# Sparse attention on one core: the first sum of W_v formed three units earlier, and its first block loaded through another queue

## The chip, the core and the metric

The kernel runs on one core of a Trainium2 chip. The metric is the device time of one execution in microseconds (us). Of the version before, three timed executions are shown: 629.04, 630.61 and 632.04 us, a median of 630.61 us. One further execution was profiled; it took 627.51 us, of which the trace covers a span of 625.8 us.

## The reference

`x` has 2708 rows of 1024 numbers, `adj` is a 2708 x 2708 matrix of zeros and ones with about 0.15% ones, so a node has some four neighbours. All is float32.

```python
h = jnp.maximum(_layernorm(x, axis=-1), 0.0)
q = h @ W_q.T + b_q
k = h @ W_k.T + b_k
v = h @ W_v.T + b_v
z = (q @ k.T) / sqrt(1024) * adj
z = jnp.where(z == 0.0, -10000.0, z)
x = x + jax.nn.relu(softmax(z, axis=1) @ v)
```

Since a row of `adj` is nearly empty, the softmax needs only the few neighbours of a node. And since the weights of a row sum to one, `v` need not be formed for every node: the neighbours' rows of `h` are summed with their weights, and the sum is multiplied by `W_v` once.

## The kernel before, in words

**Tiles and units.** The nodes are 22 tiles of 128 rows. First TensorE forms M, the product of W_q and W_k with the scale (until about 107 us). Then come 20 units. A unit multiplies two tiles of rows (256 x 1024) by a 1024 x 1024 matrix that lies in SBUF, with Strassen's scheme in Winograd's form: seven block products instead of eight. Units 0 to 9 (kind "q", the last is `last_q`) multiply `h` by M, units 10 to 19 (kind "o") multiply the weighted sums by W_v; a last single tile follows. `FIRST` is 4. Rows are gathered in an order sorted by the number of neighbours, first from unit 4 on; until unit 3 tiles come as they lie.

**The matrix.** `M[:, i, j]` are the four blocks of the matrix and `T[:, k]` (the tile `wlow`) are four sums of blocks. For W_v the names in the code are b11 = `M[:, 0, 0]`, t1 = `M[:, 0, 1]`, b21 = `M[:, 1, 0]`, b22 = `M[:, 1, 1]`. "W_v's first sum" is t1 = W_v(0,1) - W_v(0,0): the block W_v(0,0) is loaded into t1's place, ScalarE negates it there in two halves, and a DMA of GpSimd's queue adds W_v(0,1) on its way in. T1 is then T0 - t1, T2 is T1 - b11, T3 is b21 - T1. A q unit reads `M[:, 0, 0]` and `T[:, 0]` in its first two products and never reads `M[:, 0, 1]`: an o unit reads `M[:, 0, 1]` in the product where a q unit reads `T[:, 0]`. Until the change, `M[:, 0, 1]` of the old matrix has one late reader: the sum of its squares (`squared(1)`, step "g1"), a check on the size of M.

**A unit in order of time** (`multiply`, `opened`, `between`): product s2 x T1 into the bank Y, a12 x b21 into X, s4 x b22 into Z, s3 x T2 into Y; then the next unit is *opened*: its a11 x b11 into a fresh X, a ScalarE copy of X into its Y bank (the line `nc.scalar.copy(Y, X)`), its s1 product into its Z; then this unit's a22 x T3 into the old Y. Between s3 x T2 and a22 x T3 the result c22 is read out of Y: by VectorE itself (line 1097) in units 6 to 9, by a ScalarE copy (`taken`, line 1081) in units 4 and 5 and in the o units. The a22 product cannot start before that read is over.

**The attention stream.** From unit 4 on VectorE works beside the products on the attention: scores (line 863: one neighbour's row times the query's row, summed), weights, and weighted sums (line 923). The neighbours' rows `g` come by indirect DMA of GpSimd's queue from `h_dram` (line 610), the queries' rows `pq` by line 612 or 833. A buffer is refilled when VectorE has done with it. Before that the neighbour table has to be sorted: eight "puts" (line 626, steps "w0-7") write its rows to DRAM, a load of SyncE's queue brings them back (line 638).

**What sets the order.** VectorE's order is written out by hand all along: steps at the places `after(i)`, i from 0 to 6, of each unit, a table `steps_at`, and an allowance of us of attention work for each place. ScalarE's is written out until unit 4 and left to the scheduler after it; `tc.issue_after(x)` binds a step behind another. GpSimd's order is written out between some points (`pooled`). The DMA queues of SyncE, ScalarE and GpSimd are issued in the order of these engines. The finished sums go to `u_dram` through ScalarE's queue and come back as rows `or` in quarters (line 700) through SyncE's.

Of the kernel before, what the change touches and what calls it, by code (L numbers as in the profile page):

```python
# [14 lines left out]
AF = mybir.ActivationFunctionType  # L15
ALU = mybir.AluOpType
AX = mybir.AxisListType

P = 128
NB = 512  # L20
# [3 lines left out]
SLOTS = 16  # L24
# [41 lines left out]
def tile_preln_masked_attention(  # L66
# [686 lines left out]
    placed = []  # L753

    def banks_for(row):

        return_ = []
        for h in range(NH):
            return_.append(psum.tile([P, NB], FT, tag="acc", name=f"ps{h}"))
            nc.scalar.copy(return_[h], row[:, h * NB:(h + 1) * NB])  # L760
        return return_

    def natural_rows(n):
# [23 lines left out]
    steps_ahead = {(1, 5): "o1"}  # L787
# [228 lines left out]
    def opened(n):  # L1016

        if n not in banks_of:
            return
        X, Z = banks_of[n]  # L1020
        ops = ops_of[n][0]
        add_block(X, ops["a11"], M[:, 0, 0])
        Y = psum.tile([P, NB], FT, tag="acc", name="psy")
        nc.scalar.copy(Y, X)
        if n == FIRST:
            follow("o0")
        products.append(add_block(Z, ops["s1"], T[:, 0] if units[n][0] == "q" else M[:, 0, 1]))
        p5 = small("p5")
        nc.scalar.copy(p5, Z)
        opened_of[n] = Y, p5  # L1030

    def between(n):

        if n == len(units) - 1:
            single["first"] = one_started(single["banks"], single["turned"][:, 0:4, :])
        else:
            opened(n + 1)
        if n == last_q - 1:
            nc.sync.dma_start(T[:, 0], of_wv(1, 1))
            nc.sync.dma_start(M[:, 0, 0], of_wv(0, 0))  # L1040

# [8 lines left out]
    def multiply(n, results, after):  # L1050
# [8 lines left out]
        u2 = small("u2")  # L1059
        nc.scalar.copy(u2, Y)  # L1060
        after(2)
# [132 lines left out]
    def of_wv(i, j):  # L1194

        return wv[j][:, i * 4:(i + 1) * 4, :]
# [7 lines left out]
    def load_rows(unit):  # L1204
        kind, *pair = unit
        rows = []
        for t in pair:
# [4 lines left out]
            if kind == "q":  # L1212
                gather(rows[-1], h_dram[:, :], t, SLOTS, P)
            else:
                assert t in done, (t, done)
                if t in faced_tiles:
                    by_quarters(rows[-1], u_dram[t * P:(t + 1) * P, :])
                else:
                    nc.sync.dma_start(rows[-1], u_dram[t * P:(t + 1) * P, :])
# [17 lines left out]
    for n, unit in enumerate(units):  # L1237
# [15 lines left out]
        def after(i):  # L1253
# [17 lines left out]
            b11, t1, b21, b22 = M[:, 0, 0], M[:, 0, 1], M[:, 1, 0], M[:, 1, 1]  # L1271
            for at, place, src in (((-2, 0), t1, of_wv(0, 0)), ((0, 3), b21, of_wv(1, 0))):
                if (n - last_q, i) == at:
                    nc.sync.dma_start(place, src)
            if (n - last_q, i) == (0, 4):
                for h in range(2):
                    nc.scalar.copy(b22[:, 2 * h:2 * h + 2], T[:, 0, 2 * h:2 * h + 2])
            if (n - last_q, i) == (-2, 6):
                for h in range(2):
                    nc.scalar.activation(t1[:, 2 * h:2 * h + 2], t1[:, 2 * h:2 * h + 2], AF.Copy, scale=-1.0)  # L1280
                nc.gpsimd.dma_start(t1, of_wv(0, 1), accum_op=ALU.add)
            for at, place, a, b in (((0, 3), T[:, 1], T[:, 0], t1), ((1, 0), T[:, 2], T[:, 1], b11),
# [43 lines left out]
            if (n, i) == (3, 4):  # L1326
                searched()
            if (n, i) == (3, 6):
                for s in range(8, HIGH):
# [250 lines left out]
```

## Time and profile before

| | |
|---|---|
| timed runs | 629.04, 630.61, 632.04 us (median 630.61) |
| profiled execution | 627.51 us, span 625.8 us |
| granted TensorE clock | 0.999 |
| TensorE busy with matmuls | 618.9 us of the span, 1571 instructions |
| VectorE / ScalarE / GpSimd busy | 526.4 / 290.4 / 366.9 us |
| moved by DMA | 183.24 MB, mean 293 GB/s |

A float32 matmul of 512 columns is two instructions. A row of a timeline shows the start, the time, the engine and line, the operation, what is written and read, how many were merged, and in brackets how long the engine was idle before it and what ended that. "SPq" and "ACTq" are the DMA queues of SyncE and ScalarE; GpSimd's DMAs stand as POOL. A chain of waits that follows the last instruction back is nearly all TensorE here.

### The profile page before, as it was taken

The numbers are of one execution on the slowest core, as the hardware profiler recorded it, in microseconds if no ns is written. First come the engines' busy times: TensorE is split into PE (matmuls) and PEld (weight loads), VectorE is DVE, ScalarE is ACT, GpSimd is POOL, SyncE is SP. The second block draws the span as 40 slices with busy tenths as digits, with TensorE's granted clock in tenths as the row PEclk, the third lists the DMA queues.
The fourth block names the chain that finished last, engine by engine and source line by source line (L and its number), as shares of the span: only waits on it lengthen the run. The fifth ranks groups of instructions, "written<-read, shape, count | busy, mean of one in ns | idle before, by whom it ended". The sixth has DMA issues, their size and how long they took to land.

```text
span 625.8 us, 6069 instructions
## 1 busy us (share of the span) xinstructions
PE 618.9 (99%) x1571; PEld 310.0 (50%) x1571; DVE 526.4 (84%) x1024; ACT 290.4 (46%) x421; POOL 366.9 (59%) x394
## 2 busy tenths in 40 slices
PE   9999999999999999999999999999999999999996
PEld 5777767444444444444444444444444444444442
DVE  5999878988988947979898998999988899898541
ACT  3538985749677372433331532443442433432300
POOL 2649870786668577856654342767577657752421
PEclk9999999999999999999999999999999999999999
DMA  8999998688797559997696999999999999995571
GB/s 331 407 369 323 340 356 317 211 265 322 251 369 278 171 166 364 349 321 250 212 374 193 368 340 311 282 332 328 347 341 343 335 306 340 293 293 139 149 254 71
DMA packets 65952, 183.24 MB, mean 293 GB/s; under 512 B 10055, under 2 KB 20631, under 8 KB 65272
## 3 DMA queue, kind: packets, MB, share of 16 engines
q0 software_dynamic: 26656, 86.02, 43.8%
q1 hardware_dynamic: 32026, 71.53, 32.7%
q10 hardware_dynamic: 7230, 25.25, 10.4%
q8 instruction: 14, 0.23, 0.1%
q14 instruction: 26, 0.21, 0.1%
HBM read 147.23 MB, written 43.88 MB: 305 GB/s over the span
## 4 chain that ended last, share of the span: by engine, by line
PE 99%; POOL 0%; DVE 0%; POOLq 0%; issue 0%
PE ps L1011 46%; PE psy L1011 33%; PE ps_y L476 7%; PE ps_x L476 4%; PE ps_z L476 4%; PE pt L415 3%; PE ps_y L511 1%; PE ps_h L1230 0%; PE ps_v L594 0%; DVE y_alone L1396 0%; POOL out_dram L1380 0%; POOLq L1402 0%; POOL hsum L121 0%; PE ps_in L678 0%; PE ps_all L680 0%
## 5 line engine op out<-in xcount | busy, mean ns | idle before, releaser
L610 POOL DMA_INDIRECT g<-h_dram,tab x93 | 120.0, 1290 | 60.6 <-issue 20.0
L1011 PE MATMUL ps<-M,a 128*128 128x512 f32 x320 | 144.0, 593 | 0.0
L1011 PE MATMUL psy<-wlow,s 128*128 128x512 f32 x320 | 143.9, 592 | 0.0
L863 DVE SCALAR_TENSOR_TENSOR junk<-g,pq 128x1024 uint8<-128x1024 f32 x92 | 112.3, 1220 | 9.6 <-DMA g<-h_dram,tab 7.9
L1011 PE MATMUL ps<-M,s 128*128 128x512 f32 x240 | 107.9, 592 | 0.0
L1011 PEld LDWEIGHTS ps<-M,a 128*128 128x128 f32 x320 | 60.0, 190 | 72.2 <-issue 71.3
L1011 PEld LDWEIGHTS psy<-wlow,s 128*128 128x128 f32 x320 | 60.0, 190 | 72.1 <-issue 70.6
L923 DVE SCALAR_TENSOR_TENSOR u<-g,coef,u 128x1024 f32<-128x1024 f32 x70 | 89.8, 1283 | 7.0 <-ACT u L912 5.6
L389 DVE FIND_INDEX8 at<-ones,adj 128x8 uint32<-128x685 f32 (+1 forms) x88 | 74.5, 864 | 0.0
L1011 PEld LDWEIGHTS ps<-M,s 128*128 128x128 f32 x240 | 45.5, 190 | 57.2 <-issue 56.5
L1011 PE MATMUL psy<-wlow,a 128*128 128x512 f32 x160 | 72.0, 593 | 0.0
L368 ACT ACTIVATE sized<-adj 128x2708 uint8<-128x2708 f32 (+1 forms) x22 | 54.2, 2466 | 7.3 <-DMA adj<-in_adj_dram 6.0
L298 POOL TENSOR_TENSOR hsum<-hsum,x 128x256 f32<-128x256 f32 (+1 forms) x56 | 38.7, 732 | 26.5 <-DVE wlow L444 22.4
L1115 POOL DMA_INDIRECT y<-in_x_dram,tab x19 | 32.6, 1714 | 32.2 <-ACT y L1132 16.6
L1011 PEld LDWEIGHTS psy<-wlow,a 128*128 128x128 f32 x160 | 30.3, 190 | 38.6 <-issue 37.1
L808 POOL DMA_INDIRECT out_dram<-y,tab x21 | 27.0, 1284 | 16.0 <-issue 13.9
L1011 PE MATMUL ps<-wlow,s 128*128 128x512 f32 x80 | 36.1, 593 | 0.0
L944 ACT COPY v<-u 128x1024 f32<-128x1024 f32 x20 | 20.9, 1044 | 32.3 <-DVE u L923 24.8
L912 ACT ACTIVATE u<-g,coef 128x1024 f32<-128x1024 f32 x16 | 18.4, 1148 | 28.8 <-DVE coef L911 23.5
L626 POOL DMA_INDIRECT tab_dram<-tab,pos_i x22 | 21.6, 982 | 13.7 <-DVE pos_i L689 8.2
L276 ACT ACTIVATE x<-x,r 128x1024 f32<-128x1024 f32 (+1 forms) x22 | 25.8, 1232 | 5.1 <-POOL r L266 5.1
L760 ACT COPY ps<-bp_sb 128x512 f32<-128x512 f32 x42 | 24.6, 595 | 7.7 <-DVE y L1150 7.0
(253 smaller groups left out, 841.1 us busy)
## 6 DMA issues: line engine op xcount, KB each, us to landing
adj<-in_adj_dram SPq DMA_DIRECT2D x21, 1354.0 KB, 11.1
x<-in_x_dram SPq DMA_DIRECT2D x21, 512.0 KB, 11.0
h_dram<-x ACTq DMA_DIRECT2D x21, 512.0 KB, 7.2
u_dram<-v ACTq DMA_DIRECT2D x20, 512.0 KB, 7.3
or<-u_dram SPq DMA_DIRECT2D x80, 128.0 KB, 10.0
q_late<-q SPq DMA_DIRECT2D x12, 512.0 KB, 5.6
pq<-q_late POOLq DMA_DIRECT2D x12, 512.0 KB, 10.2
M<-in_wv_dram SPq DMA_DIRECT2D x3, 1024.0 KB, 15.9
```

Of the source, the lines that this page charges most:

```text
L276: nc.scalar.activation(xs[i][:n], xs[i][:n], AF.Relu, bias=r[:n, 4, i:i + 1], scale=r[:n, 3, i:i + 1])
L298: small.append(nc.gpsimd.tensor_add(hsum[:n, cols], hsum[:n, cols], xt[:n, cols]))
L368: nc.scalar.activation(sized[:n], a[:n, :, :PW], AF.Abs, accum_out=total[:n, t:t + 1])
L389: nc.vector.max_index(at[:n, k - first_k, g, :], ones[:n, 0:8], a[:n, g, :])
L476: mm = nc.tensor.matmul(bank, a_tile(o + H * a[0], a[1], i), b(o), start=first and o == 0, stop=(o == H - 1), skip_group_check=True)
L610: return nc.gpsimd.indirect_dma_start(out=dst, out_offset=None, in_=src, in_offset=off, bounds_check=N - 1, oob_is_err=False)
L760: nc.scalar.copy(return_[h], row[:, h * NB:(h + 1) * NB])
L808: to = nc.gpsimd.indirect_dma_start(out=out, out_offset=bass.IndirectOffsetOnAxis(ap=ptab.bitcast(U32)[:n, t, SLOTS:SLOTS + 1], axis=0), i ...
L863: chained(lambda: nc.vector.scalar_tensor_tensor(junk, g_of[t][s], 1.0, tq[t], op0=ALU.mult, op1=ALU.mult, accum_out=zall[:, t, s:s + 1]))
L923: chained(lambda: nc.vector.scalar_tensor_tensor(u, g_of[t][s], coef[:, s:s + 1], u, op0=ALU.mult, op1=ALU.add))
L1011: mm = nc.tensor.matmul(bank, a[:, c, :], b[:, c, :], start=False, stop=(c == 3), skip_group_check=True)
L1115: return nc.gpsimd.indirect_dma_start(out=y[:n], out_offset=None, in_=x, in_offset=off, compute_op=ALU.add)
```

## The change

Two transfers of W_v's blocks go elsewhere.

1. The load of W_v(0,0) into t1's place leaves SyncE's queue (unit 7, `after(0)`) for ScalarE's queue in unit 3, behind the copy `u2`. The negation goes from unit 7 to unit 3, and the adding DMA, on GpSimd's queue, from among the gathers of `g` in unit 7 to the place right behind the last gather of `qr` in unit 3 and ahead of the eight puts. So that `M[:, 0, 1]` is free by then, its squares (g1) are taken at the end of the opening of unit 3; those of `M[:, 0, 0]` (g0) go behind unit 4's opening instead.
2. The load of b11 = W_v(0,0) into `M[:, 0, 0]` leaves SyncE's queue, where it stood behind the load of T0 (`between`, unit 8), for ScalarE's queue, right behind the copy of X that follows the block's last reader.

```diff
     def banks_for(row):
...
-            nc.scalar.copy(return_[h], row[:, h * NB:(h + 1) * NB])
+            bank_at.append(nc.scalar.copy(return_[h], row[:, h * NB:(h + 1) * NB]))
...
-                (3, 1): "i21", (3, 3): "p21", (3, 4): "j21 c0", (3, 5): "g0", (3, 6): "w0-7 g1 g2 g3 g4", (4, 4): "b0"}
+                (3, 1): "i21", (3, 3): "p21", (3, 4): "j21 c0", (3, 6): "w0-7 g0 g2 g3 g4", (4, 4): "b0"}
...
         nc.scalar.copy(Y, X)
+        if n == last_q:
+            nc.scalar.dma_start(M[:, 0, 0], of_wv(0, 0))
...
         opened_of[n] = Y, p5
+        if n == FIRST - 1:
+            follow("g1")
...
             nc.sync.dma_start(T[:, 0], of_wv(1, 1))
-            nc.sync.dma_start(M[:, 0, 0], of_wv(0, 0))
...
-        nc.scalar.copy(u2, Y)
+        copied_at.append(nc.scalar.copy(u2, Y))
...
-                gather(rows[-1], h_dram[:, :], t, SLOTS, P)
+                rows_at.append(gather(rows[-1], h_dram[:, :], t, SLOTS, P))
...
-            for at, place, src in (((-2, 0), t1, of_wv(0, 0)), ((0, 3), b21, of_wv(1, 0))):
-                if (n - last_q, i) == at:
-                    nc.sync.dma_start(place, src)
+            if (n - last_q, i) == (0, 3):
+                nc.sync.dma_start(b21, of_wv(1, 0))
...
-            if (n - last_q, i) == (-2, 6):
-                for h in range(2):
-                    nc.scalar.activation(t1[:, 2 * h:2 * h + 2], t1[:, 2 * h:2 * h + 2], AF.Copy, scale=-1.0)
-                nc.gpsimd.dma_start(t1, of_wv(0, 1), accum_op=ALU.add)
...
+            if (n, i) == (3, 2):
+                with tc.issue_after(copied_at[-1].ins):
+                    nc.scalar.dma_start(t1, of_wv(0, 0))
+            if (n, i) == (3, 5):
+                with tc.issue_after(bank_at[-1].ins):
+                    for h in range(2):
+                        nc.scalar.activation(t1[:, 2 * h:2 * h + 2], t1[:, 2 * h:2 * h + 2], AF.Copy, scale=-1.0)
+                with tc.issue_after(rows_at[-1].ins):
+                    nc.gpsimd.dma_start(t1, of_wv(0, 1), accum_op=ALU.add)
```

The instructions of TensorE and VectorE keep their order. ScalarE, unit 3, from the copy of X at the opening of unit 3 (first row) to the one at the opening of unit 4 (last row); `sized` counts a tile's neighbours, `junk_m` is the square of a block of M. Before:

```order
L1024 COPY psy<-ps_1258 128x512
L1029 COPY p_1337<-ps_1260 128x512
L1105 COPY q_1190<-psy 128x512
L368 ACTIVATE sized,total<-adj_159 128x2708
L368 ACTIVATE sized,total<-adj_161 128x2708
L1060 COPY u_1366<-psy 128x512
L1094 COPY q_1355<-ps_1258 128x512
L760 COPY ps_1373<-bp_sb 128x512
L718 COPY a_1446<-pt 128x512
L375 ACTIVATE junk_m,msq<-M 128x1024 x2
L1024 COPY psy<-ps_1373 128x512
```

The same stretch of ScalarE with the change:

```order
L1026 COPY psy<-ps_1258 128x512
L1033 COPY p_1337<-ps_1260 128x512
L375 ACTIVATE junk_m,msq<-M 128x1024 x2
L1110 COPY q_1190<-psy 128x512
L368 ACTIVATE sized,total<-adj_161 128x2708
L1065 COPY u_1370<-psy 128x512
L1330 DMA M<-in_wv_dram 128x2048
L1099 COPY q_1359<-ps_1258 128x512
L718 COPY a_1451<-pt 128x512
L1334 ACTIVATE M<-M 128x1024 x2
L1026 COPY psy<-ps_1378 128x512
```

The squares moved up before the copy of q, the load came in behind the copy of u, and the negation (L1334) stands where two squares stood.

GpSimd's queue with the change, unit 3, from the last gathers of rows `qr` to the memsets behind the puts:

```order
L612 DMA qr_1587<-h_dram,tab 128x1024
L612 DMA qr_1589<-h_dram,tab 128x1024
L1336 DMA M<-in_wv_dram 128x2048
L626 DMA tab_dram_70<-tab,pos_i 1024x18 x8
L1341 MEMSET g_1438 128x256 x4
```

Before, the adding DMA stood later on the same queue, among the gathers of neighbours (L1281):

```order
L610 DMA g_1426<-h_dram,tab 128x1024
L610 DMA g_1427<-h_dram,tab 128x1024
L1281 DMA M<-in_wv_dram 128x2048
L610 DMA g_1428<-h_dram,tab 128x1024
L612 DMA pq_1840<-q_dram,tab 128x1024
```

It moved ahead by the eight puts, the memsets and some twenty gathers. With it a wait moved: GpSimd's DMAs take turns on eight semaphores, and the last of the eight puts now takes the turn after the adding DMA, so it waits until that has landed.

SyncE's queue before, units 8 and 9: the row quarters `or`, then T0 (L1039), then b11 (L1040), then a store of q, then b21:

```order
L700 DMA or_2262<-u_dram 32x4x256
L700 DMA or_2267<-u_dram 32x4x256 x4
L1039 DMA wlow<-in_wv_dram 128x2048
L1040 DMA M<-in_wv_dram 128x2048
L1090 DMA q_late<-q_2155 128x1024
L1274 DMA M<-in_wv_dram 128x2048
```

With the change b11 (L1028) stands on ScalarE, at the opening of unit 9, and is no longer on SyncE:

```order
L1026 COPY psy<-ps_2248 128x512
L1028 DMA M<-in_wv_dram 128x2048
L1033 COPY p_2291<-ps_2250 128x512
L946 COPY v_2304<-u_2231 128x8x4x32
L948 DMA u_dram<-v_2304 128x1024
```

More of the change, by code (lines that the diff above doesn't have):

```diff
@@ L753, in tile_preln_masked_attention @@
     placed = []
+    bank_at, rows_at, copied_at = [], [], []
     def banks_for(row):
```

## The prediction

> **What bounds the kernel now.** I read the page's busy times first, then TensorE's timeline, then what VectorE waits for.
>
> ```profile
> PE 618.9 (99%) x1571; PEld 310.0 (50%) x1571; DVE 526.4 (84%) x1024; ACT 290.4 (46%) x421; POOL 366.9 (59%) x394
> L1011 PE MATMUL psy<-wlow,s 128*128 128x512 f32 x320 | 143.9, 592 | 0.0
> ```
>
> TensorE has work in 99% of the span and no idle time ahead of its products. Since its ends are modelled, the starts tell more. Units 9 and 10, TensorE's timeline:
>
> ```profile
> 361.11 3.60 PE L1011 MATMUL ps<-M,a 128*128 128x512 f32 x8
> 364.54 3.60 PE L1011 MATMUL ps<-M,s 128*128 128x512 f32 x8
> 368.08 3.70 PE L1011 MATMUL psy<-wlow,a 128*128 128x512 f32 x8
> 371.62 3.60 PE L1011 MATMUL psy<-wlow,s 128*128 128x512 f32 x8
> ```
>
> A product takes 364.54 - 361.11 = 3.43 us from start to start. The next two take 3.54 each: 2 x 0.11 = 0.2 us of waiting around 368, hardly more in this execution. It is the place that tells most, because of what stands before it on VectorE. Its reads of c22 in units 6, 7 and 9:
>
> ```profile
> 289.27 0.68 DVE L1097 TENSOR_TENSOR q<-psy,p 128x512 f32<-128x512 f32 x1
> 315.00 0.68 DVE L1097 TENSOR_TENSOR q<-psy,p 128x512 f32<-128x512 f32 x1
> 367.34 0.69 DVE L1097 TENSOR_TENSOR q<-psy,p 128x512 f32<-128x512 f32 x1
> ```
>
> and the products on TensorE that write the same bank, of units 6 and 7 (that of unit 9 is 368.08 above):
>
> ```profile
> 290.65 3.60 PE L1011 MATMUL psy<-wlow,a 128*128 128x512 f32 x8
> 316.44 1.88 PE L1011 MATMUL psy<-wlow,a 128*128 128x512 f32 x4
> ```
>
> The reads end 0.70, 0.76 and 0.05 us before these products start. So from 239 to 368 us VectorE is a second bound beside TensorE, with under a microsecond to spare at three points: a VectorE that is late by more holds TensorE. What makes it late, in its timeline:
>
> ```profile
> 238.87 1.23 DVE L863 SCALAR_TENSOR_TENSOR junk<-g,pq 128x1024 uint8<-128x1024 f32 x1 [3.47 <-DMA g<-h_dram,tab]
> 271.79 1.23 DVE L863 SCALAR_TENSOR_TENSOR junk<-g,pq 128x1024 uint8<-128x1024 f32 x1 [3.83 <-DMA g<-h_dram,tab]
> ```
>
> Two waits for gathered neighbours, 7.3 us, both ahead of the three tight points. The profiled execution took 627.51 us, 1.7 outside the span; the three timed ones are 1.5 to 4.5 us longer, the median 3.1. A VectorE later by a few us would give such times, but no row shows that it was.
>
> **The first sum's load, part one: what leaves.** SyncE's queue and the adding DMA on GpSimd's, with the gather behind it and its time to landing:
>
> ```profile
> 226.56 0.52 SPq L1274 DMA_DIRECT2D M<-in_wv_dram  x1
> 258.54 1.02 POOL L1281 DMA_DIRECT2D M<-in_wv_dram  x1
> 259.87 1.69 POOL L610 DMA_INDIRECT g<-h_dram,tab  x1 [0.30 <-ACT w L872]
> M<-in_wv_dram POOLq DMA_DIRECT2D x1, 1024.0 KB, 12.3
> ```
>
> The stages in which they run (us, busy times, clock, DMA share, GB/s), and the ones they go to:
>
> ```profile
> 197.00:206.00 9.00, 9.00 (x33) 4.73 (x32) 7.87 (x21) 5.13 (x8) 8.54 (x13) 1.00 0.40 141
> 214.00:226.00 12.00, 12.00 (x41) 6.21 (x40) 9.59 (x13) 9.15 (x19) 9.56 (x15) 1.00 0.17 52
> 226.00:236.00 10.00, 10.00 (x24) 4.37 (x23) 1.92 (x5) 4.84 (x10) 7.05 (x12) 1.00 0.89 281
> 258.00:271.00 13.00, 13.00 (x38) 6.25 (x37) 9.82 (x19) 3.83 (x6) 8.47 (x7) 1.00 1.03 340
> ```
>
> Both leave full stages (0.89, 1.03) for empty ones (0.40, 0.17). At 281 GB/s the megabyte of 226.56 is 3.7 us of the DMA engines, just when the first neighbours come; VectorE can win between nothing and its wait of 3.47, I take 2. The adding DMA lands at 258.54 + 12.3 = 270.8, and VectorE's wait of 3.83 ends at 271.8 on a gather; the one issued next behind it stood in the same queue. I take the whole 3.8 (bounds 0 and 3.83). VectorE would be 5.8 us earlier, at most until it waits for TensorE instead.
>
> **Part two: what arrives in unit 3.** ScalarE's timeline, then TensorE's, then GpSimd's:
>
> ```profile
> 187.43 0.58 ACT L1029 COPY p<-ps 128x512 f32<-128x512 f32 x1 [1.35 <-PE ps L1011]
> 190.86 0.58 ACT L1105 COPY q<-psy 128x512 f32<-128x512 f32 x1 [2.85 <-PE psy L1011]
> 196.40 0.57 ACT L1060 COPY u<-psy 128x512 f32<-128x512 f32 x1
> 206.39 1.06 ACT L375 ACTIVATE junk_m<-M 128x1024 uint8<-128x1024 f32 x1
> 208.54 0.19 ACT L375 ACTIVATION_READ_ACCUMULATOR junk_m<-M 128x1 f32 x1
> 209.78 0.57 ACT L1024 COPY psy<-ps 128x512 f32<-128x512 f32 x1 [1.06 <-PE ps L1011]
> 231.97 2.00 ACT L1280 ACTIVATE M<-M 128x1024 f32<-128x1024 f32 x2 [3.76 <-DMA M<-in_wv_dram]
> 217.60 3.60 PE L1011 MATMUL psy<-wlow,s 128*128 128x512 f32 x8
> 208.13 1.06 POOL L612 DMA_INDIRECT qr<-h_dram,tab  x1 [0.31 <-issue]
> 214.30 1.01 POOL L626 DMA_INDIRECT tab_dram<-tab,pos_i  x1 [5.12 <-DVE pos_i L689]
> 223.28 0.97 POOL L626 DMA_INDIRECT tab_dram<-tab,pos_i  x1 [0.30 <-issue]
> ```
>
> The two squares take 208.73 - 206.39 = 2.34 us. Put behind 188.01 they end at 190.35, in the idle time before 190.86: nothing. Without that idle they would hold the copy of q by 2.34. The load is issued at about 197.0. It takes between 5.4 us (226.56 to 231.97, the earlier load of this block) and 15.9 (b11's, below), so it lands between 202.4 and 212.9; the stage is 0.40 busy, so I take 204 to 206. The negation (2.00) then fills the place of the two squares from 206.4 and ends at 208.4, before the copy due at 209.78. At the late bound it ends at 214.9 and that copy at 215.5, still before 217.60, where its bank is first used. What queues behind the negation on ScalarE are that copy and those of p and q. TensorE loses nothing.
>
> The adding DMA goes out behind the last gather at 209.2, where GpSimd is idle 5.12 us: its 1.02 us cost nothing. It delays what comes after it in one way: the last put (223.28) waits until it has landed, and the table's reload and all gathers stand behind that put. With 12.3 us it lands at 221.5, in time; at the late bound 214.9 + 12.3 = 227.2, and the attention starts 3.9 us later, which eats two thirds of the 5.8. I take 0. ScalarE's 2.00 us at 231.97, and the `taken` copy behind them, become free: cover, no time.
>
> **b11.** SyncE's queue, the time to landing of the second of these, and ScalarE's copy behind which it goes:
>
> ```profile
> 344.13 0.35 SPq L1039 DMA_DIRECT2D wlow<-in_wv_dram  x1
> 344.53 0.55 SPq L1040 DMA_DIRECT2D M<-in_wv_dram  x1
> M<-in_wv_dram SPq DMA_DIRECT2D x1, 1024.0 KB, 15.9
> 340.70 0.57 ACT L1024 COPY psy<-ps 128x512 f32<-128x512 f32 x1 [4.08 <-PE ps L1011]
> ```
>
> It lands at 344.53 + 15.9 = 360.4; the product that reads it starts at 361.11. That is the fourth tight point, 0.7 us. On ScalarE it is issued at 341.3, 3.2 us earlier, and lands by 357.2 even if it takes 15.9 again, by 346.7 if 5.4: 4 to 14 us to spare. The issue costs ScalarE some 0.5 us (the row on SyncE) in an idle stretch. What it displaces:
>
> ```profile
> 341.00:349.00 8.00, 8.00 (x20) 3.54 (x19) 7.86 (x9) 1.91 (x3) 6.34 (x6) 1.00 1.02 284
> 349.00:361.00 12.00, 12.00 (x29) 5.32 (x28) 11.16 (x23) 7.24 (x11) 1.93 (x2) 1.00 1.03 414
> ```
>
> From 341 to 349 the DMA engines are full with gathers and rows; a megabyte more at 284 GB/s puts these back by up to 3.7 us (bounds 0 and 3.7; what leaves 349 to 361 comes back later). VectorE in lead absorbs that; without a lead it meets the 0.05 us of unit 9. [...]
>
> **The sum.** On TensorE's path in the profiled execution: 627.51 less the 0.2 us seen at 368 is 627.3; all other terms are cover (5.8 us of lead for VectorE, 3.2 us for b11) that this execution does not need. What the timed runs need of it is unknown: of the median's 3.1 us over the profiled time, none (then 630.4) or all (627.5 - 0.2 = 627.3). Neither end has a row of its own; two unrelated pairs of engines sit within 0.8 us of holding TensorE, so part of it is likely, and I take half: **629.0 us**, 0.25% faster. About 0.5%, 3.2 us here, is what a measurement of this kernel can tell from no change; the forecast is within it.
>
> **Rivals.**
> - *Hidden anyway*: the timed runs are longer for a reason outside these waits. For it: TensorE without idle time even at the tight points. Against it: those margins. 630.4 us.
> - *All of it*: the timed runs lose their 3.1 us at units 6 to 10, and the lead removes that. For it: three reads with under 0.8 us. Against it: waits that happened to fit in the one execution seen. 627.3 us, 0.5% faster.
> - *b11 in front of the gathers*: the slower one. Where the lead is not won, b11's megabyte makes VectorE late by up to 3.7 us between 341 and 349, and unit 9's read of c22 passes on all but 0.05: 630.6 + 3.6 = 634.2 us. It decides from the point where the displaced time exceeds the lead. [...] Against it: VectorE waits for no gather between 340 and 368 in this trace, so these have margin.
>
> **How the numbers follow.** Forecast 0.46, hidden anyway 0.26, all of it 0.19, b11 in front 0.09. The second lies within 0.5% of 630.61 like the first, together 0.72; the third is at the bound and counts as faster, 0.19; the fourth as slower, 0.09. The range goes from 627.3, the floor of the sum, past 630.4 to 631.6: the last is 630.4 with a third of b11's 3.6. It leaves out most of the fourth and some of the first's scatter.
>
> **What would show it.** Right: the negation between 206 and 209, the adding DMA near 209, the last put still near 223; VectorE's waits of 3.47 and 3.83 shrunk or gone and its reads of c22 in units 6, 7 and 9 some us ahead of the products; b11 landed well before 361; 3.43 us from start to start all along. Wrong: a put that waits for the adding DMA, a wait of VectorE for gathers or rows between 340 and 368, a stretched product in unit 4 behind the copy of X, or timed runs that stay at 630.6 although every margin has grown: then the 3.1 us are not these waits.

## The result, and the profile after

| | before | with the change |
|---|---|---|
| median of 22 timed runs each | 629.93 us (628.32 to 634.25) | 633.44 us (630.00 to 635.27) |
| profiled execution | 627.51 us, span 625.8 | 632.40 us, span 630.7 |
| granted TensorE clock, profiled execution | 0.999 | 0.995 |

The ratio is 1.0043 (95% interval 1.0031 to 1.0054): 0.43% slower, just inside the half per cent that a measurement of this kernel can tell from no change, but 1.8 us beyond the upper end of the predicted range and 4.4 us from the forecast.

The predicted lead is there, and it is useless, because the time went elsewhere. TensorE's timeline at the border of units 3 and 4, with the change:

```profile
197.42 3.60 PE L1013 MATMUL ps<-M,s 128*128 128x512 f32 x8
204.41 1.94 PE L415 MATMUL pt<-ident,qr 128*128 128x128 f32 x8 [3.39 <-DMA qr<-h_dram,tab]
206.15 4.41 PE L1013 MATMUL psy<-wlow,s 128*128 128x512 f32 x8
210.39 1.04 PE L415 MATMUL pt<-ident,qr 128*128 128x128 f32 x8
211.26 3.60 PE L1013 MATMUL ps<-M,a 128*128 128x512 f32 x8
```

The first transposes of unit 4 wait 3.39 us for the gathered rows `qr`. Before the change no such wait stood there:

```profile
197.53 3.60 PE L1011 MATMUL ps<-M,s 128*128 128x512 f32 x8
200.96 1.04 PE L415 MATMUL pt<-ident,qr 128*128 128x128 f32 x8
205.27 1.04 PE L415 MATMUL pt<-ident,qr 128*128 128x128 f32 x8
```

With it the transposes and the product behind them are stretched: from the transposes to the next ones 210.39 - 204.41 = 5.98 us pass, where some 4.3 are usual. Busy times by stage (us, instructions, clock, DMA share, GB/s) say why:

```profile
197.00:200.00 3.00, 3.00 (x9) 1.33 (x7) 0.70 (x2) 2.63 (x5) 1.94 (x2) 1.00 1.06 431
200.00:204.40 4.40, 1.02 (x3) 0.21 (x2) 4.37 (x10) 1.01 (x2) 4.38 (x8) 1.00 1.00 412
204.40:207.80 3.40, 3.39 (x10) 2.41 (x11) 3.06 (x18) 3.02 (x4) 3.40 (x6) 0.50 0.43 172
207.80:214.00 6.20, 6.20 (x22) 3.27 (x21) 4.42 (x12) 2.49 (x3) 4.64 (x7) 1.00 0.57 182
```

The column behind the five engines is TensorE's granted clock: 0.50 for 3.4 us right after the wait, full again afterwards. And up to the wait's end the DMA engines are full (1.06, 1.00). Wait and half clock together are 3.39 + (5.98 - 4.34) = 5.0 us; 4.34 is the same distance in an execution without half clock, shown further down. TensorE's a22 product of unit 6 starts 5.0 us later than before (295.66 below, 290.65 before): the whole loss is made by then, and this is its only place.

What stands ahead of that gather, in the timelines of ScalarE with its DMA queue and of GpSimd:

```profile
184.24 0.34 ACTq L283 DMA_DIRECT2D h_dram<-x  x1
195.63 2.46 ACT L368 ACTIVATE sized<-adj 128x2708 uint8<-128x2708 f32 x1
195.64 0.35 ACTq L1330 DMA_DIRECT2D M<-in_wv_dram  x1
198.09 0.57 ACT L1065 COPY u<-psy 128x512 f32<-128x512 f32 x1
197.76 1.08 POOL L612 DMA_INDIRECT qr<-h_dram,tab  x1 [5.85 <-PE ps L1013]
199.14 0.96 POOL L612 DMA_INDIRECT qr<-h_dram,tab  x1 [0.30 <-ACT q L1099]
```

The load of W_v(0,0) is issued at 195.64, two microseconds ahead of the gather. The packets in the trace, summed by queue in GB/s per microsecond, show the order in which the bytes moved:

```
us from   GpSimd's (qr)   SyncE's   ScalarE's (load)
198              0           418            0
199              0           176          287
200              0            53          369
201             41             8          377
202            365             0           16
203            418             0            0
204            225           197            0
```

The load's packets run from 199.2 to 202.7; those of the two gathers (one for each tile of unit 4) from 201.7 to 205.1. TensorE's wait, which is for the first of the two, ends at 204.41. But the stores of h (184.24) and with them the gather are also some 4 us later than in the profile of before:

```profile
180.39 0.34 ACTq L283 DMA_DIRECT2D h_dram<-x  x1
193.51 1.08 POOL L612 DMA_INDIRECT qr<-h_dram,tab  x1 [2.70 <-DMA h_dram<-x]
```

That is not the change's doing: the first instruction that it moves on ScalarE comes at 190. The experiments had to separate the two.

The other parts went as forecast in kind. VectorE's reads of c22 in units 6, 7 and 9, and the products that write the same bank:

```profile
289.92 0.68 DVE L1102 TENSOR_TENSOR q<-psy,p 128x512 f32<-128x512 f32 x1
315.85 0.68 DVE L1102 TENSOR_TENSOR q<-psy,p 128x512 f32<-128x512 f32 x1
369.74 0.69 DVE L1102 TENSOR_TENSOR q<-psy,p 128x512 f32<-128x512 f32 x1
...
295.66 3.60 PE L1013 MATMUL psy<-wlow,a 128*128 128x512 f32 x8
321.45 3.60 PE L1013 MATMUL psy<-wlow,a 128*128 128x512 f32 x8
372.98 2.31 PE L1013 MATMUL psy<-wlow,a 128*128 128x512 f32 x5
```

Margins of 5.06, 4.92 and 2.55 us, where 0.70, 0.76 and 0.05 stood before. By themselves they do not show the lead: TensorE is 5 us late here, and the reads are no earlier than before (289.27, 315.00, 367.34). An execution of the change on chip 0, of which more below, does show it. Unit 6 there:

```profile
285.07 0.68 DVE L1102 TENSOR_TENSOR q<-psy,p 128x512 f32<-128x512 f32 x1
290.82 3.60 PE L1013 MATMUL psy<-wlow,a 128*128 128x512 f32 x8
```

The read comes 4.2 us earlier than before, the product 0.17 us later. The negation, the adding DMA and the last put, in the first execution again:

```profile
211.51 2.00 ACT L1334 ACTIVATE M<-M 128x1024 f32<-128x1024 f32 x2
213.82 0.99 POOL L1336 DMA_DIRECT2D M<-in_wv_dram  x1 [0.48 <-ACT M L1334]
226.70 0.96 POOL L626 DMA_INDIRECT tab_dram<-tab,pos_i  x1 [0.30 <-issue]
```

The last put waits for nothing (0.30 is the distance of all puts), and TensorE waits for nothing else in the middle of the program. All three are 3 to 5 us later than forecast (206.4, 209.2 and 223); in the execution on chip 0 they start at 206.67, 208.98 and 221.86.

### The profile page after: what moved, and what is told of

It is laid out like the page before. It is cut to its first block, busy times and chain, and to the rows that moved or that the text cites. A ratio compares the mean times of both kernels' runs of the same rounds, so it can differ in the third digit from the quotient of the medians.

```text
span 630.7 us, 6069 instructions
## 1 busy us (share of the span) xinstructions
PE 620.3 (98%) x1571; PEld 311.1 (49%) x1571; DVE 526.9 (84%) x1024; ACT 292.5 (46%) x421; POOL 369.0 (59%) x394
## 4 chain that ended last, share of the span: by engine, by line
PE 98%; DMA 1%; POOL 0%; DVE 0%; issue 0%; POOLq 0%
PE ps L1013 45%; PE psy L1013 33%; PE ps_y L476 7%; PE ps_x L476 4%; PE ps_z L476 4%; PE pt L415 3%; DMA qr<-h_dram,tab 1%; PE ps_y L511 1%; PE ps_h L1235 0%; PE ps_v L594 0%; DVE y_alone L1405 0%; POOL out_dram L1389 0%; POOLq L1411 0%; POOL hsum L121 0%; PE ps_in L678 0%
## 5 line engine op out<-in xcount | busy, mean ns | idle before, releaser
L610 POOL DMA_INDIRECT g<-h_dram,tab x93 | 121.3, 1305 | 65.2 <-DVE u L925 22.5
L476 PE MATMUL ps_y<-wlow 128*128 128x512 f32 x64 | 27.6, 592 | 0.0
```

Of the source, the lines that this page charges most:

```text
L476: mm = nc.tensor.matmul(bank, a_tile(o + H * a[0], a[1], i), b(o), start=first and o == 0, stop=(o == H - 1), skip_group_check=True)
L610: return nc.gpsimd.indirect_dma_start(out=dst, out_offset=None, in_=src, in_offset=off, bounds_check=N - 1, oob_is_err=False)
```

## The experiments

Theory A: the megabyte of W_v(0,0) in unit 3 moves through the DMA engines ahead of or between the gathers of `qr`, and TensorE waits for these. Its rivals: b11 on ScalarE's queue (B); the 4 us by which ScalarE was late in the profiled execution, a chance (C); the squares, the negation or the adding DMA in their new places (D). Kernels of one group ran on the same chip beside runs of the kernel before.

**Each half alone, the load later, the load added (chip 1).** The first kernel is the one before with this edit alone:

```diff
+        if n == last_q:
+            nc.scalar.dma_start(M[:, 0, 0], of_wv(0, 0))
...
-            nc.sync.dma_start(M[:, 0, 0], of_wv(0, 0))
```

> The kernel before with one half of the change: b11 is loaded by ScalarE's queue at the opening of unit 9; the first sum stays where it was. Theory A (in the changed kernel the load of M01 in unit 3 delays the gather of rows `qr` for unit 4, TensorE stands idle about 3.5 us and then runs about 3.4 us at half its granted clock): nothing of that is here, so the time is that of before within 0.2%, the first transposes of unit 4 wait for nothing, mean granted clock as before. Theory B (b11 in front of the gathers of units 8 and 9 makes VectorE late): 0.3 to 0.6% slower than before, with a wait of VectorE for gathers or rows between 341 and 368 us.

The second is the changed kernel with that edit taken back:

> The changed kernel with the other half alone: the first sum is moved to unit 3, b11 is loaded on SyncE's queue behind T0 as before. Theory A: as slow as the changed kernel, 0.3 to 0.55% over before, with the wait of the first transposes of unit 4 for `qr` (1 us or more) and a granted clock under 1 in the stage after it. Theory B: the time of before or up to 0.3% under it. Theory C (the 3.4 us wait was a chance of the one execution that was profiled, made by the stretch from 176 to 180 us in which the DMA engines moved few bytes and all of ScalarE's work came some 4 us late): no wait for `qr` here where ScalarE's stores of h stand at 180.4 as before; the time then says where else the 2.7 us are.

The third is the changed kernel with the load of W_v(0,0) behind the landing of the first rows:

```diff
-            if (n, i) == (3, 2):
-                with tc.issue_after(copied_at[-1].ins):
-                    nc.scalar.dma_start(t1, of_wv(0, 0))
+            if (n, i) == (3, 4):
+                nc.scalar.dma_start(t1, of_wv(0, 0))
```

> The changed kernel, except that the load of M01 is issued some 10 us later, behind ScalarE's copies of the first transposed rows of unit 4 (so behind the landing of the first rows `qr`); squares, negation, adding DMA and b11 keep the places of the change. Theory A: the wait at unit 4's first transposes is gone or under 0.5 us, and the time falls to that of before or below (0 to 0.5% under before); a rest may stay if the megabyte meets the next `qr` gathers at 206 to 210 us. Theory D (the two squares, put 16 us earlier on ScalarE, make the copies behind them late and these make TensorE late): still 0.3 to 0.55% over before, since the squares stay.

The fourth is the kernel before with these three lines of the change put in:

```diff
+            if (n, i) == (3, 2):
+                with tc.issue_after(copied_at[-1].ins):
+                    nc.scalar.dma_start(t1, of_wv(0, 0))
```

> The kernel before with one megabyte more: the load of M01 into its buffer in unit 3, on ScalarE's queue at the place of the change, and again at its old place on SyncE's queue (the second overwrites the first; outputs are unchanged). Squares, negation, adding DMA and b11 stay as before. Theory A: this load alone makes the loss, 0.3 to 0.55% over before, with the wait for `qr` in unit 4's first transposes. Theories B and D: the time of before within 0.2%. If ScalarE's stores of h stand at 180.4 and the wait for `qr` is there all the same, theory C falls.

| kernel | median, us | ratio to before (95%) | first store of h | first gather of `qr` | wait for it |
|---|---|---|---|---|---|
| before | 630.66 | | | | |
| b11 alone | 630.29 | 0.9999 (0.9983 to 1.0014) | 184.63 | 198.07 | 1.56 |
| first sum alone | 634.05 | 1.0057 (1.0037 to 1.0077) | 184.05 | 197.64 | 3.61 |
| load behind the rows | 631.14 | 1.0011 (0.9987 to 1.0035) | 184.66 | 198.00 | 1.53 |
| load added | (see below) | | 184.26 | 198.07 | 3.71 |

TensorE's timeline with b11 alone:

```profile
202.94 1.06 PE L415 MATMUL pt<-ident,qr 128*128 128x128 f32 x8 [1.56 <-DMA qr<-h_dram,tab]
203.84 3.60 PE L1011 MATMUL psy<-wlow,s 128*128 128x512 f32 x8
207.28 1.04 PE L415 MATMUL pt<-ident,qr 128*128 128x128 f32 x8
```

and with the first sum alone:

```profile
204.42 1.94 PE L415 MATMUL pt<-ident,qr 128*128 128x128 f32 x8 [3.61 <-DMA qr<-h_dram,tab]
206.16 4.18 PE L1013 MATMUL psy<-wlow,s 128*128 128x512 f32 x8
210.18 1.04 PE L415 MATMUL pt<-ident,qr 128*128 128x128 f32 x8
```

As the cause of the loss B falls: the time with b11 alone is that of before within 0.17%. The loss is in the first sum. But the trace with b11 alone has the wait that B named, in small (VectorE, then TensorE at unit 9):

```profile
357.64 0.71 DVE L705 STREAM_TRANSPOSE a<-or 128x512 f32<-128x512 f32 x1 [1.34 <-DMA or<-u_dram]
370.62 3.70 PE L1011 MATMUL psy<-wlow,a 128*128 128x512 f32 x8 [0.58 <-DVE q L1098]
```

Two later kernels that move b11 without the first sum show the first of these waits too (1.06 and 1.08 us), one of them also the second (0.84 us); in the profile of before and in all those with the first sum moved neither is there. So b11 on ScalarE's queue may put the row quarters back a little, and the lead covers that; it is not shown, because the kernel before was not profiled in the course that these traces took. And the expectation of e1 was wrong in a useful way: a wait of 1.56 us is there without the load, because in all four executions ScalarE's stores of h stood at 184 to 185 as in the profile of the changed kernel. So there are two courses of unit 3, and the one profile of before on which the prediction was built had the early one (stores at 180.39). In the late course the load makes 1.56 into 3.61. The wait of 1.56 left the clock alone (1.00 from 202.90 to 206.30; 202.94 to 207.28 is 4.34 us); that of 3.61 cost 5.76 - 4.34 = 1.4 us more in half clock. By these two rows the load costs 3.61 - 1.56 + 1.4 = 3.5 us, and the medians differ by 3.4. That they agree so well is partly luck: some timed runs of the kernel before have the half clock too, as is shown further down.

With the load behind the rows the wait is 1.53 again though the squares have stayed, which speaks against D. That kernel's timed runs scatter up to 637; the profiled execution was the slowest of its twelve (637.37 us), and in it TensorE had a second wait, later and for something else:

```profile
202.95 1.06 PE L415 MATMUL pt<-ident,qr 128*128 128x128 f32 x8 [1.53 <-DMA qr<-h_dram,tab]
260.80 6.33 PE L1013 MATMUL psy<-wlow,s 128*128 128x512 f32 x8 [4.17 <-ACT u L1065]
```

There ScalarE stood idle for 6.53 us ahead of its copy of u with no release that the trace explains; what that is stays open.

The kernel with the load added was a failure of its edit. It puts W_v(0,0) into the block before the sum of that block's squares is taken, and the program went on into its general path (the long loops that follow; 7108 us), so its time says nothing. Up to there unit 4 ran as usual, and its row shows the wait of 3.71 us with nothing of the change but the load. With its stores at 184.26 it belongs beside the 1.56 of the first kernel. (That the early overwriting is why the general path was taken is argued from the order of the two, not shown.)

**No load, half a load, stores first (chip 2).** The first is the changed kernel without the three lines of the load:

> The changed kernel without the load of M01 in unit 3: nothing else differs (squares, negation, adding DMA and b11 stay where the change has them). The block that is then negated and added to is not W_v's, so the output is not the reference's; the work of every engine is the same but for one megabyte. Theory A (the megabyte beside the gather of `qr` is the loss; without it the first transposes of unit 4 still wait about 1.5 us, as in two executions without it): wait for `qr` 1.5 to 1.6 us or none, no stretch at half clock, time that of before within 0.25%. Theory D (squares, negation or the adding DMA in their new places make the loss): 0.3 to 0.55% over before, with the wait of 3.4 us and more.

The next exchanges, in the list of steps, the scaling of three h tiles and their stores with a `sized` pass of ScalarE, on the kernel before with b11 on ScalarE; the one after it does so on the changed kernel:

```diff
-                ... (2, 3): "p17 a8 k8 z", ...
+                ... (2, 3): "a8 k8 p17 z", ...
```

> The kernel before with b11 on ScalarE's queue (which alone changed no time) and with one exchange in unit 2: ScalarE's scaling of the last three h tiles and their stores go in front of one `sized` pass of 2.46 us, not behind it. If the gather of `qr` waits for these stores, which the five late profiles suggest (stores at 184.1 to 184.7, gather 13 us behind the first of them), it is issued up to 2.46 us earlier and unit 4's wait of 1.56 us goes: 1 to 1.6 us faster than before (0.15 to 0.25%). If the wait does not matter in the runs that are timed, or something else holds the gather: the time of before within 0.1%.

> The changed kernel with the same exchange: stores of h in front of one `sized` pass. Theory A says the load of M01 then finds the gather issued up to 2.46 us earlier: the wait for `qr` falls from 3.4 or 3.6 us to about 1.1, the half clock behind it goes, and the time falls by 2 to 3 us, to 630.5 to 631.5. If the load is as much earlier as the gather is and still goes in front of it in the DMA engines, the wait falls only to what the load adds (1.5 to 2 us).

The last loads half of W_v(0,0) at the place of the change and half behind the copies of unit 4's first transposed rows:

> The changed kernel with the load of M01 cut in two: the first half (512 KB) at the place of the change, the second behind ScalarE's copies of unit 4's first transposed rows. Theory A is a matter of bytes in front of the gather: the wait lies halfway between 1.55 (none there) and 3.5 (a megabyte), 2.4 to 2.7 us, and the time about 1 us over before, or 2 if the half clock comes already with such a wait. If the gather is late for another reason, the wait stays at 3.4 or falls to 1.5.

| kernel | median, us | ratio to before (95%) | first store of h | first gather of `qr` | wait for it |
|---|---|---|---|---|---|
| before | 629.91 | | | | |
| change without the load | 631.14 | 1.0013 (0.9995 to 1.0031) | 184.44 | 198.12 | 2.39 |
| stores first | 632.47 | 1.0032 (1.0014 to 1.0049) | 181.43 | 190.61 | none |
| change, stores first | 633.99 | 1.0057 (1.0030 to 1.0085) | 182.67 | 194.76 | 2.02 |
| change, half load | 630.68 | 1.0000 (0.9980 to 1.0019) | 184.33 | 197.88 | 2.27 |

Without the load the changed kernel is within 0.25% of before, as A expected, and the interval includes no change; D is left with 0.13%, at most 0.31% by the interval. Against the expectation its wait was 2.39 us, not 1.5, and a stretch at half clock followed (0.68 on average from 203.50 to 206.90; 203.59 to 209.63 is 6.04 us). So such a wait has a scatter of about a microsecond of its own, and half a load (2.27) can't be told from none by this row, nor by time: its ratio is 1.0000, its interval of 0.2% either way holds the 1 us that was expected.

The exchange shows that the place is held from two sides. The gather goes out at 190.61 and TensorE waits for no rows, yet the kernel is slower. TensorE's timeline with the stores first:

```profile
211.81 0.24 PE L678 MATMUL ps_in<-sort,before 128*128 128x144 bf16 x1 [1.84 <-DVE sort L666]
...
213.13 5.40 PE L1011 MATMUL ps<-wlow,s 128*128 128x512 f32 x8 [1.03 <-DVE s L722]
```

Now it waits 1.84 and 1.03 us for VectorE, first for its sort, and runs at half clock again (0.55 on average from 213.00 to 216.40). VectorE's search waits for the adjacency's last block until 203.19, where with b11 alone it was 199.58:

```profile
203.19 0.09 DVE L389 MATCH_VALUE_LOAD at<-ones,adj 128x8 f32 x1 [4.15 <-DMA adj<-in_adj_dram]
```

The `sized` pass that was put back starts at 184.08, where with b11 alone it starts at 180.91, and so frees its adjacency buffer 3.2 us later. That the last block is late because it is loaded into that buffer is argued, not shown. My expectation had priced only the engine on which the exchange was made. On the changed kernel the wait fell to 2.02, not to 1.1, and the time did not fall at all; its runs scatter from 629 to 641 us.

**A megabyte taken out of the stage (chip 14).** SyncE's two stores of unit 2's q rows go behind those of unit 3, in the first kernel on the one before (with b11 on ScalarE), in the second on the change:

```diff
-            (nc.scalar if t < 4 else nc.sync).dma_start(dst, q)
             formed.add(t)
+            if t in (4, 5):
+                later.append((dst, q))
+                return
+            sent_q = (nc.scalar if t < 4 else nc.sync).dma_start(dst, q)
+            if t == 7:
+                with tc.issue_after(sent_q.ins):
+                    for d, held_q in later:
+                        nc.sync.dma_start(d, held_q)
```

> The kernel before with b11 on ScalarE's queue (which alone changed no time) and SyncE's two stores of unit 2's q rows, 1 MB issued at 184.9 and 191.7, put behind those of unit 3 (about 204 us). From 188 to 197 us the DMA engines were full (share 0.99) with these stores, the stores of h for which the gather of `qr` waits, and the last blocks of the adjacency. If bytes ahead of that gather set its time, 1 MB less at some 390 GB/s is up to 2.7 us: unit 4's wait of 1.56 us goes, the half clock that sometimes follows it too, and nothing on ScalarE or VectorE is put back (which is what cost the exchange of stores and `sized` its gain): 1 to 2 us faster than before (0.15 to 0.3%). If the gather is held by something else: the time of before within 0.1%, wait 1.5 us or more.

> The changed kernel with the same two stores behind those of unit 3. The load of M01 then takes the place of a megabyte that has left: the wait for `qr` falls from 3.4 us to 0.7 to 1.9, too short for the half clock or just at it, and the time is that of before within 0.2%. If the load costs by its place directly in front of the gather and not by the bytes of the whole stage, the wait stays over 3 us and the time 0.3 to 0.55% over before.

The first gave 629.40 us against 629.46, ratio 0.9992 (0.9971 to 1.0012): nothing. Its gather still went out at 197.88, with a wait of 1.43; the last packets of h's stores moved between 196 and 197 us, as they did with b11 alone, so the bytes of the stage alone do not hold the gather. The second gave 628.96, ratio 0.9978 (0.9962 to 0.9995), with 12 of 13 runs between 628.5 and 629.7 us; its profiled execution was the thirteenth (633.07 us), with a wait of 2.75 us and the half clock (0.65 on average from 205.00 to 208.40), where 0.7 to 1.9 us and none had been expected.

**Again, beside the change (chips 9 and 0).** The last kernel and the change on chip 9; both, and the change without the load, on chip 0:

> The kernel of the last experiment (the change, with unit 2's two stores of q rows behind those of unit 3) a second time, to see whether its 0.2% over before hold and to have an execution of the common kind: 12 of its 13 runs lay between 628.5 and 629.7 us with a clock of 0.998, the profiled one at 633.1 with 0.996. If the megabyte that has left the stage is what counts: again 0.1 to 0.4% faster than before, a wait for `qr` of less than 2 us, no stretch at half clock. If the first result was chance: within 0.1% of before.

> The changed kernel once more, beside the one above on the same chip: 0.3 to 0.55% over before, a wait for `qr` of 3 us and more, a clock of 0.995 in nearly all runs. A wait under 2 us with the same time would leave the cause open.

> The changed kernel, on one chip with the two below. The loss has been 0.18% on a chip where ScalarE's stores of h stood at 180.4 in the profile, and 0.43 to 0.57% where they stood at 184 to 185. If that place decides: with stores near 180.4 a wait for `qr` of about 1.3 us, no half clock, 0.1 to 0.3% over before; with stores past 184 a wait of 3.4 us or more, half clock, 0.3 to 0.6% over before.

> The changed kernel with unit 2's two stores of q rows behind those of unit 3. If a megabyte less ahead of the gather makes up for the one that the change adds: between 0.25% under and 0.1% over before on this chip, and 0.1 to 0.5% under the changed kernel beside it, more where ScalarE is late.

> The changed kernel without the load of M01 (its output is not the reference's, since the block that is negated is another one). Theory A: the time of before within 0.2%, and below the changed kernel by what that loses here; a rest over 0.2% would belong to the squares, the negation or the adding DMA.

| kernel | chip | median, us | ratio to before (95%) | first store of h | first gather of `qr` | wait for it |
|---|---|---|---|---|---|---|
| before | 9 | 626.94 | | | | |
| change | 9 | 627.76 | 1.0018 (1.0001 to 1.0035) | 180.36 | 193.92 | 1.30 |
| change, q stores later | 9 | 627.36 | 1.0006 (0.9995 to 1.0017) | 180.14 | 191.36 | none |
| before | 0 | 627.25 | | | | |
| change | 0 | 627.90 | 1.0002 (0.9986 to 1.0018) | 180.03 | 192.36 | 0.75 |
| change, q stores later | 0 | 627.11 | 0.9993 (0.9981 to 1.0006) | 180.79 | 192.59 | none |
| change without the load | 0 | 627.32 | 0.9994 (0.9978 to 1.0009) | 181.66 | 194.11 | none |

On these chips all five profiled executions took the early course (on chips 1, 2 and 14 all ten took the late one), and the kernel before is 2 to 4 us faster than on the three others. So the change missed its expectations here: 0.3 to 0.55% over before and 3 us of waiting had been forecast for chip 9, and on chip 0 even the branch for the early course had 0.1 to 0.3%. TensorE's timeline of the change on chip 0:

```profile
201.21 1.06 PE L415 MATMUL pt<-ident,qr 128*128 128x128 f32 x8 [0.75 <-DMA qr<-h_dram,tab]
202.11 3.60 PE L1013 MATMUL psy<-wlow,s 128*128 128x512 f32 x8
205.55 1.04 PE L415 MATMUL pt<-ident,qr 128*128 128x128 f32 x8
```

and without the load:

```profile
198.08 3.60 PE L1013 MATMUL ps<-M,s 128*128 128x512 f32 x8
201.51 1.04 PE L415 MATMUL pt<-ident,qr 128*128 128x128 f32 x8
```

The rows that show the mechanism most directly are those of the first gather itself. Kernels that move other transfers in this stage are left out:

| first gather of `qr`, us | without the load | half a load | with the load |
|---|---|---|---|
| late course: from issue to its first packet | 1.79 to 1.80 (3 executions) | 2.26 | 3.39 to 3.89 (3) |
| late course: from issue to the end of TensorE's wait | 4.87 to 5.47 (3) | 5.48 | 6.65 to 6.78 (3) |
| early course: from issue to landing | 5.97 and 6.64 | | 8.65 and 8.72 |

In the early course the load adds 2.0 to 2.75 us to the gather's time, about what a megabyte takes at 412 to 431 GB/s (2.4 to 2.5 us). The landing is not in the traces of the late course; there the first packet is 1.6 to 2.1 us later.

This settles A and C together. C was half right: the late course is a condition of the chip or of the execution, not of the change. But the load has its price in both courses. Early: no wait without it (before, and the change without the load), 0.75 and 1.30 us with it, behind which the clock stayed at 1.00. Late: 1.4 to 2.4 us without it, 3.4 to 3.7 with it, and then the half clock each time. So the change, or its first half, costs 0 to 0.2% where the course is early and, if the first measurement took the course of its profile, 0.43 to 0.57% where it is late.

These are single profiles, but each timed run has its mean granted clock. In the 16 profiles of this program's normal path, 0.996 or less goes with a stretch at half clock inside the program, 0.997 or more with none (eight profiles each). By that mark 19 of the 22 timed runs of the change in the first measurement had one, and 6 of 7 of the first sum alone. Of the kernel before it was 27 of 82 on chips 1, 2 and 14, of the change without the load 6 of 12 on chip 2. Of the kernel with the stores first it was 2 of 12, so the half clock of its profile is not what makes that kernel 0.3% slower. On chips 9 and 0 it was none of 50 runs of the kernel before and 1 of 23 of the change.

Does the kernel with the later q stores beat both? Its median is under that of the change beside it on both chips (by 0.4 and 0.8 us, inside the intervals), it shows no wait for `qr` in either early execution, and the first gather lands 5.2 us after its issue in both. Against the kernel before it was 0.2% faster on chip 14, where 7 of 23 runs of the kernel before and 1 of its 13 have the mark of the half clock, and the same on two chips. The expected gain did not repeat, so that looks like the change without its loss; a gain over before is not shown.

The late course has a sign in the DMA engines too. The stage from 176 to 180 us of the changed kernel, first profile (the last two columns are DMA share and GB/s):

```profile
176.00:180.00 4.00, 4.00 (x11) 1.68 (x9) 3.73 (x18) 1.26 (x4) 2.50 (x7) 1.00 0.61 102
```

On chip 0, the same kernel:

```profile
176.00:180.00 4.00, 4.00 (x11) 1.74 (x10) 3.69 (x17) 2.35 (x4) 2.25 (x7) 1.00 1.05 386
```

In the late course ScalarE stands idle for 2.3 to 5.2 us ahead of a copy of u near 170 us, after its product has ended, and the `sized` passes behind it, the adjacency's loads and the stores of h all come later. Why it stands there is open.

## Why the prediction was wrong

**The step that failed** is "Part two: what arrives in unit 3", with its conclusion "TensorE loses nothing". Three things in it were wrong, the last decides.

- *The issue time.* "The load is issued at about 197.0", behind the copy of u. It went out at 195.64 (late course) and 193.64 (early), some 2 us before that copy ran: the DMA was issued while ScalarE was still in the `sized` pass ahead of the copy.
- *The empty stage.* "The stage is 0.40 busy, so I take 204 to 206." That mean hid a fuller first half, with a full stage just ahead. The profile of before in pieces of 4 us:

```profile
193.00:197.00 4.00, 4.00 (x10) 1.71 (x10) 2.33 (x7) 3.93 (x5) 3.18 (x4) 1.00 0.95 353
197.00:201.00 4.00, 4.00 (x11) 1.69 (x10) 3.33 (x7) 3.27 (x4) 4.00 (x7) 1.00 0.57 185
201.00:205.00 4.00, 4.00 (x17) 2.31 (x16) 3.64 (x7) 1.77 (x4) 3.84 (x6) 1.00 0.33 131
```

  Only the third piece is as empty as I took the whole. And what runs through the first two is the gather of `qr`, issued at 193.51 and needed at 200.96. The load itself landed sooner than the 204 to 206 (its last packet ended at 202.7 and, on chip 0, at 201.4): it was the gather that paid.
- *What the megabyte delays.* I asked when the load lands and who needs what it brings. I did not ask what else is under way in the DMA engines just then and who waits for that. In the execution I used, the first gather landed at 200.15 and the transposes start at 200.96, so it had 0.8 us to spare; a megabyte at the 412 to 431 GB/s of these stages is 2.4 to 2.5 us. By the prediction's own habit (a term for what is displaced, as it made for b11), the step would have had a term of 0 to 2.5 us for the gather, which it put at nothing without a reason. The runs gave 0.75 to 1.30 us early, about 2 late, and 1.4 to 1.6 more for the half clock.

**The first part** held as a mechanism and was mis-sized: of the predicted lead of 5.8 us the margins grew by 4.4, 4.2 and 2.5. The 3.8 us of the adding DMA came: no execution with the first sum moved waits more than 0.9 us for a gather near 272 us. The 2 us of the load did not: VectorE's wait near 239 us is gone in the first profile of the change, but ten of the eleven other executions with the first sum moved still have 2.3 to 4.4 us of it. The lead was called cover that the profiled execution does not need, and that was right.

**What the timed runs need of it.** The forecast gave the lead half of the 3.1 us between profile and median, for want of a row. The change without its load has the lead and not the loss: 0.9994 and 1.0013. So the lead is worth nothing that these times show, and the rival "hidden anyway" was right on this point: part of the excess of the timed runs is the late course of unit 3 (a wait for `qr` of 1.4 to 1.6 us and more in executions without the load, and the half clock in 27 of 82 runs of the kernel before), well ahead of the place where I looked for it. All of it is not accounted for. Two traces in the late course without the lead, both with b11 on ScalarE's queue, do have TensorE waiting at the tight point of unit 9, for 0.58 and 0.84 us.

**b11** held by its times: no loss, no gain. Of the slower rival, "b11 in front of the gathers", the traces without the lead show at most a small part: VectorE waits 1.06 to 1.34 us for row quarters, and TensorE up to 0.84 us, not the 3.6 us. The change was slower by the same kind of mechanism, a megabyte ahead of gathers, at the other load, where I had not put the question. The margins of the last put and of the copy of X held as well.

**The range** ended at 631.6 because its only slower case was b11's; with the bound above it would have reached 630.4 + 2.5 = 632.9, still without the half clock. (Halfway between the forecast's own ends, 627.3 and 630.4, is 628.9, not 629.0; it makes no difference.)

## What to carry to other kernels

When a transfer is moved into a stage, list the transfers under way there with their consumers and slack, and price the move as bytes over bandwidth against the smallest of these; the mean share of a stage says nothing about the microseconds that matter. One profiled execution may have taken a course that most do not: a margin under a microsecond in it is no margin. And cover for an engine that is not on the path bought nothing measurable here, while what the change displaced cost up to half a per cent: price both sides.

## What the runs showed of the hardware

- The granted clock fell to half behind TensorE's waits from 2.02 us on. Behind waits of 0.75, 1.30, 1.43, 1.53 and 1.56 us it stayed at 1.00. Behind those of 2.02, 2.27, 2.39, 2.75 and 3.39 it was 0.64, 0.58, 0.68, 0.65 and 0.50 on average in 3.4 us from about the wait's end; behind 3.61 and 3.71 it was 0.88 and 0.90 on average from 197 to 206 us, and 0.92 and 0.90 from 206 to 214. In these seven executions it cost 1.4 to 1.7 us whatever the wait's length (the 4.34 us between two sets of transposes became 5.72 to 6.04), so that the wait of 2.02 us cost nearly double. Behind the wait of 4.17 us the product took 6.33 us in place of 3.60.
- In the clock records of the change's first trace the stretch begins at 204.36 us, 0.05 us before the wait ends, and lasts 3.41 us; a second one begins at 627.61 us, 2.73 us after TensorE's last product has ended. Two waits one close behind the other, 1.84 and 1.03 us (stores first), were followed by half clock as well, the single one of 1.56 was not. That the two count together is an estimate from these two runs; it is not shown.
- Where the load and the gather overlapped (the change on chip 0, 197 to 200 us), the load of 8 KB packets moved 287, 254 and 238 GB/s and the gather of 4 KB packets 94, 115 and 176: 3.1, 2.2 and 1.4 times as much. In the change's first profile, from 199 to 200 us, the load moved 287 GB/s and SyncE's queue, in packets of 4 KB, 176. How a DMA engine shares its time between queues is not shown.
- The load, which stands behind the copy of u on ScalarE in program order, was issued 2.45 us before that copy ran (195.64 and 198.09; on chip 0 2.10 us, 193.64 and 195.74).
